# Layer 1's query projection: from fp32 to three fp32r products of split parts, with the first four tiles turned inside layer 0's feed-forward

## The chip, the core and the metric

The kernel runs on one NeuronCore of one Trainium2 chip. The core has five engines with a queue of instructions each: TensorE (PE; its weight loads are shown apart as PEld), VectorE (DVE), ScalarE (ACT), GpSimd (POOL) and SyncE (SP, which only issues DMAs here). They run side by side and wait for each other by semaphores. The metric is the device time of one execution in microseconds, as a median of several runs; less is better. A profile comes from one more execution, whose time is given beside its span.

## What is computed

Two layers work on x of 8 sequences x 112 rows x 512. Each layer adds a cross-attention to a context of 375 rows and then a gated feed-forward of width 1408. The change is about the queries of layer 1 alone:

```
x = x + L0_xattn(layernorm(x), ctx, mask)
x = x + L0_ffn(layernorm(x), w1, w2, w3)        # activations in 8 bits, weights ternary
x = x + L1_xattn(layernorm(x), ctx, mask, Wq, bq, Wk, bk, Wv, bv, Wo, bo, ...)
x = x + L1_ffn(layernorm(x), ...)               # weights are integers with a scale

# in L1_xattn
q = layernorm(x) @ Wq.T + bq                    # 896 x 512 by 512 x 512, fp32
k = ctx @ Wk.T + bk;  v = ctx @ Wv.T + bv       # 16 heads of 32
probs = softmax(clip(q k' / sqrt(32), -50, 50)) # masked
```

## The kernel before

The 8 x 112 rows are held in SBUF as 7 tiles of 128 rows, `xs[0]` to `xs[6]`. They form two groups, `GROUPS = [(0, 4), (4, 7)]`: tiles 0 to 3 (512 rows) and tiles 4 to 6 (384 rows).

Layer 0's feed-forward runs tile by tile (L561 to L611). `gate_up0(i)` (L509) makes both products from the quantized row tile in three pieces of H (512, 512, 384); ScalarE takes Silu (L521) and VectorE multiplies (L522). `ranges0(i)` finds the rows' scales: a square sum on ScalarE (L271), a maximum on VectorE (L272) and then a chain of some fifteen operations on one number per row (L275 to L282), each of which waits for the one before; its result is `q_fwd`. `round0(i)` (L541) scales on ScalarE (L543) and rounds on GpSimd in two halves (L546). `turn_down0(i)` transposes that on TensorE (L328) and copies it out on ScalarE (L330), and `down0(i)` (L553) multiplies by w3 and adds to `xs[i]` on VectorE (L559). The loop is skewed: tile i's gate_up0 stands ahead of tile i-1's turn_down0 and down0. `turn_gate0(i + 1)` transposes the next tile's quantized rows. Between these, `fill(n)` takes n steps of the keys and values of layer 1 (L181 and L190, fp32), which need only the context. A step ends with a copy out of PSUM: keys by ScalarE (L184), values by VectorE (L192).

What sets the order: TensorE and SyncE follow the order in which the program is written, everywhere. Up to `written.close()` (L612) VectorE, ScalarE and GpSimd do so too. What comes after L612 is put by a scheduler where it finds room, and can stand ahead of written code: the normalisations "ln2a" and "ln2b" of L614 and L620 appear in VectorE's queue from 145 us on.

After the loop come the queries of layer 1. `transpose2(i, ...)` (L205) writes the normalised tile `d` (L144), transposes it with four fp32 transposes (L214) and copies it by ScalarE into `h2T` (L215). `queries(g)` (L650) has four blocks `dc` of 128 outputs; each is four fp32 matmuls over the chunks `kc` of 128 inputs (L656), as wide as the group has rows, and an addition of bq on VectorE (L658) into `qT`. The order on TensorE is tiles 0 and 1, turn_down0(6), a fill, tiles 2 and 3, down0(6), then two blocks of group 0, tile 4, a block, tile 5, a block, tile 6, a fill, group 1's four blocks, and `fold_bias` (L670). Then the attention of layer 1 begins with `scores` (L811).

Memory: large tiles share seven slabs of 12 KB per partition (L71): raw weights, the quantized rows `h1`, keys and values of each sequence, `wq`, `h2T`, later the integers of layer 1's feed-forward. A slab is handed out again when its last reader is done. Layer 1's feed-forward (L935, L953) multiplies in fp32r, the type of which the change makes use; a value in it is split there into a rounded part and a rest (L753, L754 and L943, L944).

Of the kernel before, what the change touches and what calls it, by code (L numbers as in the profile page):

```python
# [42 lines left out]
NT = B * T // P  # L43
# [5 lines left out]
LN_EPS = 1e-5  # L49
# [10 lines left out]
HBLK = [(0, 512), (512, 512), (1024, 384)]  # L60


@with_exitstack
def two_layers(ctx: ExitStack, tc: tile.TileContext, x, ctxT, ctxN, mask0, mask1, w1, w2, w3,
               wq, wk, wv, wo, bq, bk, bv, bo, gamma, beta, rscale,
# [9 lines left out]
    def slab(name, dtype=F32):  # L75
        return slabs.tile([P, SLAB], dtype, name=name, tag="slab")
# [26 lines left out]

    small = [stat]

    def rsqrt(v, name):

        r, n = v.shape
        bits = small[-1].tile([P, n], I32, name=f"{name}_b", bufs=2)[:r]
        nc.vector.tensor_scalar(bits, v.bitcast(I32), 1, None, ALU.logical_shift_right)  # L110
        y = small[-1].tile([P, n], F32, name=f"{name}_y", bufs=2)[:r]
        nc.vector.tensor_scalar(y.bitcast(I32), bits, -1.0, RSQRT, ALU.mult, ALU.add)
        h = small[-1].tile([P, n], F32, name=f"{name}_h", bufs=2)[:r]
        nc.vector.tensor_scalar_mul(h, v, -0.5)
        t = small[-1].tile([P, n], F32, name=f"{name}_t", bufs=2)[:r]
        for _ in range(3):
            if n == 1:
                nc.vector.scalar_tensor_tensor(t, y, h, y, ALU.mult, ALU.mult)
            else:
                nc.vector.tensor_mul(t, y, y)  # L120
                nc.vector.tensor_mul(t, t, h)
            nc.vector.scalar_tensor_tensor(y, t, 1.5, y, ALU.add, ALU.mult)
        return y

    def moments(srcs, name):

        r = srcs[0].shape[0]
        mv = small[-1].tile([P, len(srcs), nc.vector.BN_AGGR_DIM], F32, name=f"{name}_mv", bufs=2)[:r]
        for j, src in enumerate(srcs):
            bn = small[-1].tile([P, nc.vector.BN_STATS_DIM], F32, name="bn", bufs=4)[:r]  # L130
            nc.vector.bn_stats(bn, src)
            nc.vector.bn_aggr(mv[:, j, :], bn)
        return mv

    def normaliser(srcs, name):

        mv = moments(srcs, name)
        r = srcs[0].shape[0]
        ve = small[-1].tile([P, len(srcs)], F32, name=f"{name}_ve", bufs=2)[:r]
# [58 lines left out]
    def fill(n=1):  # L198
        for _ in range(n):
            next(kv_steps, None)  # L200


    h2T = {}

    def transpose2(i, write, j, pool, psum):  # L205
        g = 0 if i < GROUPS[0][1] else 1
        i0, i1 = GROUPS[g]
        if i == i0:
            h2T[g] = slab("h2T")[:, :KC * (i1 - i0) * P].rearrange("p (k t) -> p k t", k=KC)
        h = pool.tile([P, D], F32, name="d", bufs=2)  # L210
        write(h, j)
        pt = psum.tile([P, KC, P], F32, name="s")
        for kc in range(KC):
            nc.tensor.transpose(pt[:, kc, :], h[:, kc * P:(kc + 1) * P], ident)  # L214
        nc.scalar.copy(h2T[g][:, :, (i - i0) * P:(i - i0 + 1) * P], pt)  # L215


    with tc.tile_pool(name="w0", bufs=1, side="right") as w0p, \
# [45 lines left out]
        def quantizers(srcs, n, name, squares):  # L264


            m = len(srcs)
            ss = w0p.tile([P, m], F32, name=f"{name}_ss", bufs=2)
            mx = w0p.tile([P, m], F32, name=f"{name}_mx", bufs=2)
# [7 lines left out]
            lim = w0p.tile([P, m], F32, name=f"{name}_lim", bufs=2)  # L277
            nc.vector.tensor_mul(lim, mx, r)
            nc.vector.tensor_scalar_max(lim, lim, Q_EPS)
            fwd = w0p.tile([P, m], F32, name=f"{name}_fwd", bufs=2)  # L280
            nc.vector.reciprocal(fwd, lim)
            nc.vector.scalar_tensor_tensor(fwd, fwd, 127.0, r, ALU.mult, ALU.mult)  # L282

            def back(mean, which):
                t = w0p.tile([P, m], F32, name=f"{name}_back{which}", bufs=4)
# [48 lines left out]
            q1[i] = transposed_h(q1[i], D, "q1", w0p)  # L334


        with tc.tile_pool(name="work0", bufs=2, side="right") as work0:
# [6 lines left out]

            def load_x(b0, b1):

                pool = w0p if b1 == B else work0
                t = pool.tile([T, b1 - b0, D], F32, name=f"x0_{b0}", bufs=1)
                nc.sync.dma_start(out=t, in_=x[b0:b1].rearrange("b t d -> t b d"))
                x0.extend(t[:, b, :] for b in range(b1 - b0))  # L350
# [155 lines left out]
        with tc.tile_pool(name="work1", bufs=2, side="right") as work1:  # L506
# [43 lines left out]
            def turn_down0(i):  # L550
                q3[i] = transposed_h(q3[i][0], H, "q3", work1), q3[i][1]
# [24 lines left out]
            ranges0(1, 1)  # L576
            round0(1)
            fill(1)
            for i in range(2, NT):
                gate_up0(i)  # L580
                if i == 2:
                    steps_of(2, 2)
                elif i == 3:
                    next(preparing[2])
                elif i == 4:
                    next(preparing[3])
                ranges0(i, 2)
# [36 lines left out]

# [25 lines left out]
    def queries(g):  # L650
        i0, i1 = GROUPS[g]
        cols = slice(i0 * P, i1 * P)
        for dc in range(KC):
            ps = ps_mm.tile([P, 512], F32, name="mm")[:, :(i1 - i0) * P]
            for kc in range(KC):
                nc.tensor.matmul(ps, lhsT=wq_s[:, kc, dc * P:(dc + 1) * P], rhs=h2T[g][:, kc, :],  # L656
                                 start=(kc == 0), stop=(kc == KC - 1))
# [25 lines left out]
    folding = fold_bias()  # L683
    next(folding)
    fill(1)
    for _ in queries(1):
        pass
    next(folding)
# [398 lines left out]
```

## Time and profile before

| what | us |
|---|---|
| median of three runs | 529.88 (529.83 to 530.57) |
| the profiled execution: its own time | 527.85 |
| the profiled execution: its span | 526.1 |
| mean granted clock of TensorE | 0.994 |
| L656, query products: start of the first to end of the last | 214.1 to 243.1 |
| idle ahead of L656 by the trace | 6.7, all of it weight loads waiting for their turn |
| tile 4 of layer 0's feed-forward: TensorE waits for VectorE's L316 | 1.75, at 177.4 |
| tile 3 of it: TensorE waits for VectorE's L559 | 0.73, at 150.1 |
| ScalarE ahead of L215 of tile 4: waits for L656 | 16.4, ended at 229.0 |

How to read a profile line: engine or start first, then the length in microseconds, the line of the kernel, the operation, what it writes and reads with its shape, and in brackets the idle time ahead of it with what ended it. An fp32 matmul leaves two records on TensorE, one in a shorter type leaves one. Consecutive instructions of one kind are merged ("x16"), and then the start of the next line tells better than the length when they were over. The chain of waits is followed back from the last instruction and lists the pieces of work that nothing could have shortened without something else coming last. GpSimd's times are rough.

### The profile page before, as it was taken

Reading aid. Unit: us, or ns where it says so; the run is one execution under the profiler, and the core shown is the slowest. Engines: PE = TensorE matmul, PEld = TensorE weight load, DVE = VectorE, ACT = ScalarE, POOL = GpSimd, SP = SyncE. Lnnn points to the kernel's source line nnn. Section 1 sums busy time; section 2 is a strip of 40 time slices with the busy share of each in tenths; the row PEclk is TensorE's granted clock in tenths of the full one; section 3 lists DMA queues with packets and bytes.
Section 4 is the critical chain, followed back from the end, with each engine's and each line's share of the span. In section 5 each row is a group of like instructions: output and inputs, shape, how many; then the busy total and the mean of one; then the engine's idle time right before and its main releaser. Section 6 shows DMA issues by size and latency. Waiting matters only on the chain.

```text
span 526.1 us, 8715 instructions
## 1 busy us (share of the span) xinstructions
PE 510.2 (97%) x3348; PEld 311.8 (59%) x3348; DVE 323.7 (62%) x797; ACT 246.4 (47%) x429; POOL 121.8 (23%) x218
## 2 busy tenths in 40 slices
PE   9999999999999899999989999999999999999994
PEld 6445554454554455455565465555554788889983
DVE  2552558767899767533566587796888763334432
ACT  0335747766755456013775365376565233103310
POOL 0000211111011111300551447447572430000000
PEclk9999999999999999999999999999999999999999
DMA  8998795100400100500430031011311000010001
GB/s 249 348 405 329 249 348 197 40 0 1 137 2 2 58 2 0 191 2 1 148 110 26 1 120 51 1 53 37 108 39 52 22 0 0 21 40 21 1 20 45
DMA packets 13231, 45.75 MB, mean 87 GB/s; under 512 B 1969, under 2 KB 3008, under 8 KB 12032
## 3 DMA queue, kind: packets, MB, share of 16 engines
q1 hardware_dynamic: 11744, 41.43, 23.0%
q0 software_dynamic: 1280, 3.70, 2.1%
q8 instruction: 28, 0.46, 0.3%
q14 instruction: 19, 0.16, 0.1%
q10 hardware_dynamic: 160, 0.01, 0.0%
HBM read 41.46 MB, written 1.84 MB: 82 GB/s over the span
## 4 chain that ended last, share of the span: by engine, by line
PE 81%; DVE 9%; ACT 3%; POOL 3%; DMA 2%; issue 1%; DVEq 0%; POOLq 0%; ACTq 0%
PE s L935 14%; PE mm L190 13%; PE mm L181 12%; PE down L953 7%; PE mm L517 5%; PE mm L656 5%; PE mm L407 4%; PE s L378 4%; PE mm L709 3%; PE s L811 3%; PE num L837 3%; PE mm L557 2%; PE den L832 2%; DVE e L816 2%; PE s L328 1%
## 5 line engine op out<-in xcount | busy, mean ns | idle before, releaser
L181 PE MATMUL mm<-cT,wk 128*128 128x375 f32 x256 | 88.2, 489 | 0.0
L190 PE MATMUL mm<-wv,cT 128*125 128x512 f32 x192 | 87.5, 599 | 0.0
L935 PE MATMUL s<-h4T,w 128*128 128x512 f32 (+1 forms) x352 | 72.6, 367 | 0.6 <-ACT qT L844 0.6
L816 DVE TENSOR_SCALAR e<-s,upper 125x448 f32<-125x448 f32 x96 | 59.2, 676 | 18.0 <-PE s L811 11.5
L935 PEld LDWEIGHTS s<-h4T,w 128*128 128x128 f32 x352 | 63.5, 188 | 9.2 <-PE num L837 0.9
L817 ACT ACTIVATE e<-e 125x448 f32<-125x448 f32 x96 | 52.3, 571 | 30.3 <-DVE e L816 29.7
L181 PEld LDWEIGHTS mm<-cT,wk 128*128 128x128 f32 x256 | 47.1, 192 | 28.2 <-issue 2.0
L190 PEld LDWEIGHTS mm<-wv,cT 128*125 128x125 f32 x192 | 34.5, 187 | 37.9 <-issue 36.4
L953 PE MATMUL down<-w,gu 128*128 128x512 f32 x154 | 37.0, 397 | 0.0
L517 PE MATMUL mm<-w_q,q_qT 128*128 128x512 fp8e4 (+1 forms) x168 | 34.6, 361 | 0.7 <-DVE tokens L559 0.7
L803 POOL TENSOR_TENSOR e<-e,e 125x448 f32<-125x448 f32 x28 | 32.2, 1181 | 10.9 <-PE num L837 10.9
L811 PE MATMUL s<-qT,kv 32*125 32x112 f32 x768 | 31.7, 283 | 2.5 <-DVE e L816 1.7
L788 POOL TENSOR_SCALAR w<-raw 128x640 fp32r<-128x640 int32 (+2 forms) x29 | 19.9, 690 | 56.4 <-ACT w L786 56.0
L953 PEld LDWEIGHTS down<-w,gu 128*128 128x128 f32 x154 | 28.7, 188 | 6.7
L546 POOL TENSOR_SCALAR q<-gu 128x704 bf16<-128x704 f32 x14 | 10.8, 791 | 93.1 <-ACT gu L543 93.1
L811 PEld LDWEIGHTS s<-qT,kv 32*125 32x125 f32 x768 | 26.1, 186 | 9.8 <-issue 5.5
L415 POOL DMA_DIRECT2D tokens<-x x14 | 10.7, 768 | 90.1 <-DVE x L409 62.1
L943 ACT CAST gu<-gu 128x512 fp32r<-128x512 f32 (+1 forms) x22 | 12.5, 568 | 40.0 <-DVE gu L941 40.0
L786 ACT ACTIVATE w<-raw,zero_point 128x640 fp32r<-128x640 int32 (+2 forms) x29 | 22.6, 779 | 17.1 <-DMA raw<-in_wd_dram 9.1
L941 DVE SCALAR_TENSOR_TENSOR gu<-s,su,gu 128x512 f32<-128x512 f32 (+1 forms) x22 | 15.0, 684 | 22.2 <-PE s L935 20.6
L517 PEld LDWEIGHTS <-q_qT 128*128 128x128 bf16 x168 | 16.4, 98 | 19.3 <-issue 2.1
L837 PEld LDWEIGHTS num<-e,kv 125*32 125x32 f32 x768 | 18.8, 110 | 12.8 <-issue 7.1
(211 smaller groups left out, 756.3 us busy)
## 6 DMA issues: line engine op xcount, KB each, us to landing
cT<-in_ctxT_dram SPq DMA_DIRECT2D x13, 750.0 KB, 6.7
raw<-in_w_dram SPq DMA_DIRECT2D x6, 1408.0 KB, 22.2
cN<-in_ctxN_dram SPq DMA_DIRECT2D x8, 768.0 KB, 4.9
raw<-in_wg_dram SPq DMA_DIRECT2D x8, 320.0 KB, 2.9
raw<-in_wu_dram SPq DMA_DIRECT2D x8, 320.0 KB, 3.0
raw<-in_wd_dram SPq DMA_DIRECT2D x8, 320.0 KB, 3.0
out_dram<-d SPq DMA_DIRECT2D x7, 256.0 KB, 2.0
wk<-in_wk_dram SPq DMA_DIRECT2D x4, 256.0 KB, 4.9
```

What stands on the lines that cost most here:

```text
L181: nc.tensor.matmul(ps[dc], lhsT=wk_s[:, kc, dc * P:(dc + 1) * P], rhs=cT[:, kc, :], start=(kc == 0), stop=(kc == KC - 1))
L190: nc.tensor.matmul(ps, lhsT=cT[:, kc, c * CK:(c + 1) * CK], rhs=wv_s[:, kc, :], start=(kc == 0), stop=(kc == KC - 1))
L517: nc.tensor.matmul(ps[:, :n], lhsT=qT[:, kc, :], rhs=w[:, kc * H + n0:kc * H + n0 + n], start=(kc == 0), stop=(kc == KC - 1))
L656: nc.tensor.matmul(ps, lhsT=wq_s[:, kc, dc * P:(dc + 1) * P], rhs=h2T[g][:, kc, :], start=(kc == 0), stop=(kc == KC - 1))
L786: nc.scalar.activation(t, raw, AF.Square, bias=zero_point, accum_out=squares[:, k:k + 1])
L803: add(e, e, e1)
L811: nc.tensor.matmul(ss[r][:, dc, :], lhsT=kT[rows, dc, c * CK:(c + 1) * CK], rhs=qT[rows, dc, b * T:(b + 1) * T], start=True, stop=True)
L816: nc.vector.tensor_scalar(e, ss[r], upper[:, c, b:b + 1], -CLIP, ALU.min, ALU.max)
L817: nc.scalar.activation(e, e, AF.Exp, scale=SC1)
L837: nc.tensor.matmul(num[r * HD:(r + 1) * HD, dc, :], lhsT=v[:, c, head], rhs=es[r][:CK, dc, :], start=(c == 0 and dc == 0), stop=(c == NCK ...
L935: nc.tensor.matmul(ps[:, :n], lhsT=w[:, c:c + P], rhs=h4T[k][:, kc, :n], start=(kc == 0 and k == 0), stop=(kc == KC - 1 and k == 1))
L953: nc.tensor.matmul(ps, lhsT=gus[k][:, hc, j * P:(j + 1) * P], rhs=w[:, c:c + D], start=(hc == 0 and k == 0), stop=(hc == HC - 1 and k == 1))
```

## The change

Each value of the transposed rows and of wq is split into a high part, rounded to fp32r after scaling by `LESS`, and a rest; a scaled difference of the two is a third operand. A block of queries is then high x high + low x low in one PSUM tile, and diff x diff in a second tile `less`, all fp32r: 12 matmuls for 4 fp32 ones. ScalarE takes the first tile out with scale and bias, VectorE subtracts the second.

wq is loaded one tile earlier (behind `i == 3`). At the end of tile 4 ScalarE makes `wq_high`, and GpSimd makes `wq_low` (128 x 2048, a subtraction and a scaling) and half of `wq_diff` (128 x 1024); the other half follows at the end of tile 5. The moments of tiles 0 to 3 are taken within the loop, their 1/std is worked out in tile 5 behind ranges0, and the transposes of tiles 0 and 1 stand at the end of tile 5, those of tiles 2 and 3 at the end of tile 6, ahead of turn_down0(6). All of this is in the written order. Group 1 stays behind the loop, with statistics for tiles 4 and 5 together. New buffers `wq_high`, `wq_low`, `h2T_high` and group 1's three parts get pools of their own; several small tiles get one buffer in place of two, and the last half of x moves to another pool.

```diff
+SPLIT = 2.0 ** -12
+LESS = 1.0 - 2.0 ** -13
...
-    def transpose2(i, write, j, pool, psum):
+    def write2(i, write, j, pool):
+        h2[i] = pool.tile([P, D], F32, name="d", bufs=2)
+        write(h2[i], j)
+
+    def transpose2(i, psum):
+
         g = 0 if i < GROUPS[0][1] else 1
...
         for kc in range(KC):
-            nc.tensor.transpose(pt[:, kc, :], h[:, kc * P:(kc + 1) * P], ident)
-        nc.scalar.copy(h2T[g][:, :, (i - i0) * P:(i - i0 + 1) * P], pt)
+            nc.tensor.transpose(pt[:, kc, :], h2[i][:, kc * P:(kc + 1) * P], ident)
+        j = i - GROUPS[g][0]
+        high, low, diff = (t[:, :, j * P:(j + 1) * P] for t in h2T[g])
+        nc.scalar.activation(high, pt, AF.Identity, scale=LESS)
+
+        def end():
+            nc.vector.tensor_sub(low, pt, high.bitcast(F32))
+            nc.vector.scalar_tensor_tensor(diff, high.bitcast(F32), SPLIT, low.bitcast(F32),
+                                           ALU.mult, ALU.subtract)
+        return end
...
-                pool = w0p if b1 == B else work0
+                pool = last0 if b1 == B else work0
...
+            mv2 = stat.tile([P, GROUPS[0][1], nc.vector.BN_AGGR_DIM], F32, name="mv2")
+
+            def moments2(i):
+                bn = stat.tile([P, nc.vector.BN_STATS_DIM], F32, name="bn", bufs=4)
+                nc.vector.bn_stats(bn, xs[i])
+                nc.vector.bn_aggr(mv2[:, i, :], bn)
+
+            def difference():
+
+                t = slab("h2T", F32R)
+                k = len(wq_diff) * KC // 2
+                kcs = slice(k, k + KC // 2)
+                wq_diff.append(t[:, KC * D:].rearrange("p (k d) -> p k d", d=D))
+                nc.gpsimd.tensor_sub(wq_diff[-1], wq_high[:, kcs].bitcast(F32),
+                                     wq_low[:, kcs].bitcast(F32))
+                return t[:, :KC * D].rearrange("p (k t) -> p k t", k=KC)
+
+            ending2 = []
             for i in range(2, NT):
                 gate_up0(i)
...
                 ranges0(i, 2)
                 if i == 4:
                     next(preparing[3])
+                    moments2(0)
+                    moments2(2)
+                elif i == 5:
+                    small.append(stat)
+                    ve = stat.tile([P, GROUPS[0][1]], F32, name="ln2a_ve")
+                    nc.vector.tensor_scalar_add(ve, mv2[:, :, 1], LN_EPS)
+                    rstd2 = rsqrt(ve, "ln2a")
+                    small.pop()
+
+                    def normal2(h, i):
+                        nc.vector.tensor_scalar(h, xs[i], mv2[:, i, 0:1], rstd2[:, i:i + 1],
+                                                ALU.subtract, ALU.mult)
+                    for k in range(2):
+                        write2(k, normal2, k, work1)
                 fill(2 if i < 4 else 1)
                 turn_down0(i - 1)
...
+                elif i == NT - 1:
+                    for k in range(2):
+                        ending2[k]()
+                        write2(k + 2, normal2, k + 2, work1)
                 fill(1)
                 if i < NT - 1:
                     turn_gate0(i + 1)
...
                 down0(i - 1)
                 if i == 3:
                     next(preparing[3])
-                if i == 4:
                     wq_s = slab("wq")[:, :KC * D].rearrange("p (k d) -> p k d", k=KC)
                     nc.sync.dma_start(out=wq_s, in_=wq)
+                    moments2(1)
+                elif i == 4:
+                    queried = ExitStack()
+                    qp = queried.enter_context(tc.tile_pool(name="qp", bufs=1))
+                    wq_high, wq_low, h2T_high = (qp.tile([P, KC, D], F32R, name=name)
+                                                 for name in ("wq_high", "wq_low", "h2T_high"))
+                    nc.scalar.activation(wq_high, wq_s, AF.Identity, scale=LESS)
+                    nc.gpsimd.tensor_sub(wq_low, wq_s, wq_high.bitcast(F32))
+                    nc.gpsimd.tensor_scalar(wq_low, wq_low.bitcast(F32), 1.0 / SPLIT, 1.0,
+                                            ALU.mult, ALU.mult)
+                    wq_diff = []
+                    h2T_diff = difference()
+                    moments2(3)
+                elif i == 5:
+                    h2T[0] = h2T_high, difference(), h2T_diff
+                    ending2 += [transpose2(k, ps_s) for k in range(2)]
+                elif i == NT - 1:
+                    ending2 += [transpose2(k, ps_s) for k in range(2, 4)]
+                    ending2[2]()
+                    ending2[3]()
+            turn_down0(NT - 1)
+            fill(1)
             written.close()
             small.pop()
-            write = normaliser(xs[:3], "ln2a")
-            for i in range(2):
-                transpose2(i, write, i, work1, ps_s)
-            turn_down0(NT - 1)
-            fill(1)
-            transpose2(2, write, 2, work1, ps_s)
-            write = normaliser(xs[3:5], "ln2b")
-            transpose2(3, write, 0, work1, ps_s)
             down0(NT - 1)
...
             for kc in range(KC):
-                nc.tensor.matmul(ps, lhsT=wq_s[:, kc, dc * P:(dc + 1) * P], rhs=h2T[g][:, kc, :],
+                nc.tensor.matmul(ps, lhsT=wq_high[:, kc, of], rhs=high[:, kc, :],
+                                 start=(kc == 0), stop=False)
+                nc.tensor.matmul(ps, lhsT=wq_low[:, kc, of], rhs=low[:, kc, :],
+                                 start=False, stop=(kc == KC - 1))
+            less = ps_s.tile([P, 512], F32, name="s")[:, :(i1 - i0) * P]
+            for kc in range(KC):
+                nc.tensor.matmul(less, lhsT=wq_diff[kc // 2][:, kc % 2, of], rhs=diff[:, kc, :],
                                  start=(kc == 0), stop=(kc == KC - 1))
-            nc.vector.tensor_scalar_add(qT[:, dc, cols], ps, bq_s[:, dc:dc + 1])
+            nc.scalar.activation(qT[:, dc, cols], ps, AF.Identity, bias=bq_s[:, dc:dc + 1],
+                                 scale=1.0 + SPLIT)
+            nc.vector.tensor_sub(qT[:, dc, cols], qT[:, dc, cols], less)
             yield
...
-    transpose2(4, write, 1, tailp, ps_s)
-    next(asking)
-    for i in range(5, NT):
-        transpose2(i, normaliser(xs[i:i + 1], f"ln2{i}"), 0, tailp, ps_s)
-        next(asking, None)
...
+        write = normaliser(xs[4:6], "ln2b")
+        for i in range(4, NT):
+            if i == NT - 1:
+                write = normaliser(xs[i:], "ln2c")
+            write2(i, write, i % 2, tailp)
+            transpose2(i, ps_s)()
+            next(asking, None)
```

More of the change, by code (lines that the diff above doesn't have):

```diff
@@ L104, in two_layers, with buffers @@
     small = [stat]
+    def buffers(name):
+        return 2 if name in ("q3", "ln3") else 1
     def rsqrt(v, name):
         r, n = v.shape
-        bits = small[-1].tile([P, n], I32, name=f"{name}_b", bufs=2)[:r]
+        bufs = buffers(name)
+        bits = small[-1].tile([P, n], I32, name=f"{name}_b", bufs=bufs)[:r]
         nc.vector.tensor_scalar(bits, v.bitcast(I32), 1, None, ALU.logical_shift_right)
-        y = small[-1].tile([P, n], F32, name=f"{name}_y", bufs=2)[:r]
+        y = small[-1].tile([P, n], F32, name=f"{name}_y", bufs=bufs)[:r]
         nc.vector.tensor_scalar(y.bitcast(I32), bits, -1.0, RSQRT, ALU.mult, ALU.add)
-        h = small[-1].tile([P, n], F32, name=f"{name}_h", bufs=2)[:r]
+        h = small[-1].tile([P, n], F32, name=f"{name}_h", bufs=bufs)[:r]
         nc.vector.tensor_scalar_mul(h, v, -0.5)
-        t = small[-1].tile([P, n], F32, name=f"{name}_t", bufs=2)[:r]
+        t = small[-1].tile([P, n], F32, name=f"{name}_t", bufs=bufs)[:r]
         for _ in range(3):
@@ L127, in moments @@
         r = srcs[0].shape[0]
-        mv = small[-1].tile([P, len(srcs), nc.vector.BN_AGGR_DIM], F32, name=f"{name}_mv", bufs=2)[:r]
+        mv = small[-1].tile([P, len(srcs), nc.vector.BN_AGGR_DIM], F32, name=f"{name}_mv",
+                             bufs=buffers(name))[:r]
         for j, src in enumerate(srcs):
@@ L138, in normaliser @@
         r = srcs[0].shape[0]
-        ve = small[-1].tile([P, len(srcs)], F32, name=f"{name}_ve", bufs=2)[:r]
+        ve = small[-1].tile([P, len(srcs)], F32, name=f"{name}_ve", bufs=1)[:r]
         nc.vector.tensor_scalar_add(ve, mv[:, :, 1], LN_EPS)
@@ L200, in fill @@
             next(kv_steps, None)
-    h2T = {}
-    def transpose2(i, write, j, pool, psum):
-        g = 0 if i < GROUPS[0][1] else 1
[L207 to L211, printed above, removed]
+    h2T, h2 = {}, {}
+    def write2(i, write, j, pool):
+        h2[i] = pool.tile([P, D], F32, name="d", bufs=2)
+        write(h2[i], j)
+    def transpose2(i, psum):
+        g = 0 if i < GROUPS[0][1] else 1
         pt = psum.tile([P, KC, P], F32, name="s")
         for kc in range(KC):
-            nc.tensor.transpose(pt[:, kc, :], h[:, kc * P:(kc + 1) * P], ident)
-        nc.scalar.copy(h2T[g][:, :, (i - i0) * P:(i - i0 + 1) * P], pt)
+            nc.tensor.transpose(pt[:, kc, :], h2[i][:, kc * P:(kc + 1) * P], ident)
[7 more added lines that the diff above has]
+        return end
     with tc.tile_pool(name="w0", bufs=1, side="right") as w0p, \
@@ L267, in quantizers @@
             m = len(srcs)
-            ss = w0p.tile([P, m], F32, name=f"{name}_ss", bufs=2)
-            mx = w0p.tile([P, m], F32, name=f"{name}_mx", bufs=2)
+            ss = w0p.tile([P, m], F32, name=f"{name}_ss", bufs=buffers(name))
+            mx = w0p.tile([P, m], F32, name=f"{name}_mx", bufs=buffers(name))
             for j, src in enumerate(srcs):
@@ L276, in quantizers @@
             r = rsqrt(ss, name)
-            lim = w0p.tile([P, m], F32, name=f"{name}_lim", bufs=2)
+            lim = w0p.tile([P, m], F32, name=f"{name}_lim", bufs=buffers(name))
             nc.vector.tensor_mul(lim, mx, r)
             nc.vector.tensor_scalar_max(lim, lim, Q_EPS)
-            fwd = w0p.tile([P, m], F32, name=f"{name}_fwd", bufs=2)
+            fwd = w0p.tile([P, m], F32, name=f"{name}_fwd", bufs=buffers(name))
             nc.vector.reciprocal(fwd, lim)
@@ L284, in back @@
             def back(mean, which):
-                t = w0p.tile([P, m], F32, name=f"{name}_back{which}", bufs=4)
+                t = w0p.tile([P, m], F32, name=f"{name}_back{which}",
+                             bufs=4 if name == "q3" else 1)
                 nc.vector.tensor_scalar(t, lim, mean, 1.0 / 127.0, ALU.mult, ALU.mult)
@@ L334, in turn_gate0 @@
             q1[i] = transposed_h(q1[i], D, "q1", w0p)
-        with tc.tile_pool(name="work0", bufs=2, side="right") as work0:
+        with tc.tile_pool(name="work0", bufs=2, side="right") as work0, \
+                tc.tile_pool(name="last0", bufs=1, side="right") as last0:
             m0 = load(work0, mask0, [B, S2], "m0", nc.scalar, U8)
@@ L652, in queries @@
         cols = slice(i0 * P, i1 * P)
+        high, low, diff = h2T[g]
         for dc in range(KC):
+            of = slice(dc * P, (dc + 1) * P)
             ps = ps_mm.tile([P, 512], F32, name="mm")[:, :(i1 - i0) * P]
             for kc in range(KC):
-                nc.tensor.matmul(ps, lhsT=wq_s[:, kc, dc * P:(dc + 1) * P], rhs=h2T[g][:, kc, :],
+                nc.tensor.matmul(ps, lhsT=wq_high[:, kc, of], rhs=high[:, kc, :],
[5 more added lines that the diff above has]
+                nc.tensor.matmul(less, lhsT=wq_diff[kc // 2][:, kc % 2, of], rhs=diff[:, kc, :],
                                  start=(kc == 0), stop=(kc == KC - 1))
-            nc.vector.tensor_scalar_add(qT[:, dc, cols], ps, bq_s[:, dc:dc + 1])
+            nc.scalar.activation(qT[:, dc, cols], ps, AF.Identity, bias=bq_s[:, dc:dc + 1],
+                                 scale=1.0 + SPLIT)
+            nc.vector.tensor_sub(qT[:, dc, cols], qT[:, dc, cols], less)
             yield
@@ L677, in two_layers @@
     next(asking)
-    transpose2(4, write, 1, tailp, ps_s)
-    next(asking)
-    for i in range(5, NT):
-        transpose2(i, normaliser(xs[i:i + 1], f"ln2{i}"), 0, tailp, ps_s)
-        next(asking, None)
[L683 to L688, printed above, removed]
+    with tc.tile_pool(name="g1p", bufs=1, side="right") as g1p:
+        h2T[1] = [g1p.tile([P, KC, 384], F32R, name=f"h2T1_{k}") for k in range(3)]
+        write = normaliser(xs[4:6], "ln2b")
[5 more added lines that the diff above has]
+            next(asking, None)
+        folding = fold_bias()
+        next(folding)
+        fill(1)
+        for _ in queries(1):
+            pass
+        next(folding)
+    queried.close()
+    tail2 = ctx.enter_context(tc.tile_pool(name="tail2", bufs=1, side="right"))
     sg_s = load(tailp, sg, [P, HC], "sg", nc.gpsimd)
     su_s = load(tailp, su, [P, HC], "su", nc.gpsimd)
-    h4T = [tailp.tile([P, KC, 512], F32R, name=f"h4T_{k}") for k in range(2)]
+    h4T = [tail2.tile([P, KC, 512], F32R, name=f"h4T_{k}") for k in range(2)]
     h4 = {}
```

## The prediction

> **What bounds the kernel now.** I read the page first, then the chain of waits around the queries, then the timelines of each engine over the last feed-forward tiles. From the page:
>
> ```profile
> PE 510.2 (97%) x3348; PEld 311.8 (59%) x3348; DVE 323.7 (62%) x797; ACT 246.4 (47%) x429; POOL 121.8 (23%) x218
> ...
> PE 81%; DVE 9%; ACT 3%; POOL 3%; DMA 2%; issue 1%; DVEq 0%; POOLq 0%; ACTq 0%
> ```
>
> TensorE is the bound nearly everywhere. The chain from 200 to 245 us (start, length, piece) holds nothing but TensorE:
>
> ```profile
> 211.92 2.37 PE mm L557 x11
> 214.29 6.87 PE mm L656 x16
> ...
> 225.47 3.44 PE mm L656 x8
> ...
> 232.78 10.32 PE mm L656 x32
> ```
>
> So what the queries lose in TensorE time the kernel gains, as long as no new wait stands in front. The waits must be sought in the tiles before, where the change puts its preparation. There, in the old order, VectorE and GpSimd (start, length):
>
> ```profile
> 160.16 0.77 DVE L121 TENSOR_TENSOR ln_t<-ln_t,ln_h 128x2 f32<-128x2 f32 x1
> 160.96 0.71 DVE L122 SCALAR_TENSOR_TENSOR ln_y<-ln_t,ln_y 128x2 f32<-128x2 f32 x1
> 161.71 0.16 DVE L120 TENSOR_TENSOR ln_t<-ln_y 128x2 f32<-128x2 f32 x1
> ...
> 189.77 0.16 DVE L282 SCALAR_TENSOR_TENSOR q_fwd<-q_fwd,q_y 128x1 f32<-128x1 f32 x1
> ...
> 193.26 0.75 DVE L559 SCALAR_TENSOR_TENSOR tokens<-mm,q_back,tokens 128x512 f32<-128x512 f32 x1 [3.20 <-PE mm L557]
> ```
>
> ```profile
> 160.14 1.52 POOL L546 TENSOR_SCALAR q<-gu 128x704 bf16<-128x704 f32 x2 [14.15 <-ACT gu L543]
> ...
> 191.74 1.52 POOL L546 TENSOR_SCALAR q<-gu 128x704 bf16<-128x704 f32 x2 [11.43 <-ACT gu L543]
> ```
>
> Two operations of 2 elements, worth 0.15 us, took 0.77 and 0.71: each ended with one of GpSimd's two 0.76 us instructions. One VectorE operation got in per GpSimd instruction, no more.
>
> **The queries.** Every fp32 product of L656 is two records. A block of group 0 is 8 records in 3.44 us; four blocks are 6.87 + 3.44 + 3.44 = 13.75. Group 1 is 10.32. The new products are fp32r, the type of layer 1's feed-forward, one record each:
>
> ```profile
> 417.32 34.15 PE L935 MATMUL s<-h4T,w 128*128 128x512 f32 x144
> ...
> 473.17 30.69 PE L935 MATMUL s<-h4T,w 128*128 128x384 f32 x176
> ```
>
> By the starts of what follows (451.31 and 503.70) they go at 33.99/144 = 0.236 and 30.53/176 = 0.1735 us, each with its own weight load. A group has 4 blocks x 4 chunks x 3 products = 48: 11.33 and 8.33. Gain: 2.42 + 1.99 = **4.4 us**. Transposes are as many as before (28), and down0, fill and turn_down0 keep their number.
>
> **The rest of the query stage: 0.** Counted from the first query at 0, block 0 ends at 2.8, block 1 at 5.6, tile 4's transposes at 6.1. The first eviction needs bq, which landed 5.2 us in (L658 at 219.31 waited for it) and frees block 0's bank before 6.1. VectorE has, up to tile 6's parts: the residual 0.75, two normal writes 1.1, statistics and rsqrt of tile 6 3.2, its write 0.5, four subtractions of `less` 2.8, three ends of 1.45, some 12.7 us; they must be over when group 1 begins at 11.3 + 1.3 + 3.4 = 16.0 (fold_bias's 2.8 can follow, it is needed 8.3 later). The cover is 3 us; a bad order of VectorE's free schedule costs up to 1. ScalarE sat idle 16.4 us here before and takes the evictions and fp32r copies (0.6 each). The last subtraction of `less` (0.6 to 0.7, as L658's 0.62) lies beside L670's 0.86.
>
> **Moved off older tiles: -0.9.** The old ln2a work had floated forward: a bn_stats of 0.59 at 145.29, two d writes (0.46 each) at 171.24 and a statistic at 168.05. Behind the first, TensorE waited 0.73 until L559 at 149.33; without it the quantizer's chain can start when ScalarE's accumulator is there, 146.17, not 146.47: 0.3. Behind the others, TensorE waited 1.75 for L316 before tile 5's transposes; the chain gets some 0.9 shorter of which 0.3 is the shift itself: 0.6. The new moments of tiles 0 and 2 come behind L316 and delay only PSUM copies that have about 0.5 us to spare. The wq load moves up one tile in SP's queue; it already went at 140.60, with only context loads beside it: 0.
>
> **Tile 5: +5.0, the step that decides.** All on the old clock, less 0.9. wq_high (128x2048 on ScalarE, by L543's 1.56 for 1408 about 2.1) fills an idle stretch, 178.2 to 180.3; gate_up0(5)'s first L521 behind it comes 0.1 late, and a free PSUM pair covers that. Then GpSimd gets three long instructions in one go: a subtraction of 2048, a scaling of 2048, a subtraction of 1024. By L788 (0.40 for 256, 0.73 for 640) the scaling takes 1.95. [...] The quantizer's chain of tile 5 reaches its first two-input operation at 187.0 and was worth 2.1 more. [...]
>
> ```profile
> 409.41 1.30 POOL L722 TENSOR_TENSOR tokens<-tokens,beta 128x512 f32<-128x512 f32 x1
> ```
>
> ```profile
> 409.84 1.35 DVE L850 TENSOR_TENSOR qT<-qT,e 128x448 f32<-128x448 f32 x1
> ```
>
> (L850 alone: 0.62; it ran from 410.57.) [...] Tile 1's transposes end at 197.8 to 198.2. Queued behind them on TensorE is gate_up0(6), which without waits would start at 183.85 + 2.53 + 0.61 + 2.58 + 0.22 + 2.37 + 0.87 = 193.05. That is 5.0. Lower end: 2.8 if both writes pass ahead of the second difference; 0.3 if the chain isn't held either.
>
> **Tile 6: +0.8.** L559 and the quantizer first; then two ends (0.67 + 0.75) and two writes before down0(5)'s result. Tile 3's d is ready some 1 us after TensorE asks, also with GpSimd's pair in between; behind it stands turn_down0(6), which had 0.16 to wait for GpSimd anyway. From 0.4 to 1.2.
>
> **The clock: +1.7.** A gap has a second price here (columns: PE, PEld, DVE, ACT, POOL busy, granted clock, DMA share, GB/s):
>
> ```profile
> 271.00:272.00 1.00, 0.00 (x0) 0.00 (x0) 0.89 (x2) 0.00 (x0) 0.99 (x1) 1.00 0.07 23
> 272.00:273.00 1.00, 0.53 (x3) 0.36 (x3) 1.00 (x3) 0.66 (x2) 1.00 (x2) 1.00 0.36 117
> ...
> 275.00:276.00 1.00, 1.00 (x15) 0.81 (x9) 0.41 (x1) 0.16 (x2) 1.00 (x2) 0.50 0.06 16
> 276.00:277.00 1.00, 1.00 (x2) 0.62 (x3) 1.00 (x3) 0.67 (x2) 0.82 (x2) 0.50 0.00 0
> ```
>
> After 1.7 us idle and some thin work the clock was halved for 3.4 us: 1.7 lost. [...]
>
> **Other edits: 0.** The smaller buffer counts are of names allocated once. x's last half in its own pool and the new pools only move addresses; a release waited for would cost up to 1 us, and nothing suggests a gain.
>
> **Sum.** -4.4 - 0.9 + 5.0 + 0.8 + 1.7 = +2.2: from the profiled execution's 527.85 (span 526.1 and 1.75 around it) to 530.05. The median of the runs is 2.03 above that execution; 529.88 + 2.2 = **532.1**.
>
> **The rivals.** (A) The forecast, chance 0.54, 530.9 to 534.2. (B) The same hold, but no dip behind it, or the old dip gone: +0.5, 530.4; chance 0.14. (C) Faster: GpSimd lets VectorE's two writes through ahead of the second difference. [...] For it: TensorE needs only two writes, 0.92 us. Against it: the alternation at 160.16. [...] Chance 0.23. (D) The lock hardly bites, long GpSimd work lies beside VectorE: -4.4 - 0.9 + 0.3 + 0.4 = -4.6, 525.3; speaks against it that L850 was held for nearly all of 1.3 us. Chance 0.09. That fp32r doesn't reach its rate is covered by L953, which loads other weights every time and takes 0.233.
>
> **How the numbers follow.** 0.2% is 1.06 us, about what a measurement here can tell from no change. Slower: nearly all of A and a little of B, 0.55. Same: most of B and the upper part of C, 0.18. Faster: D and most of C, 0.27. The range from 527.4 to 534.2 leaves out D, a strip of C and a strip above A.
>
> **What would show it.** Right: L656's successor takes 11.3 and 8.3 us; VectorE's small operations beside GpSimd's long ones last 2 us and more; TensorE sits idle about 5 us between tile 5's down0 and tile 6's gate_up0, with a clock of 0.5 behind it. Wrong: TensorE dense there; or a wait in the query stage, on bq or VectorE, of over 1 us.

## The result and the profile after

The changed kernel took 530.95 us (median of 21 runs) beside 529.41 us of the kernel before: ratio 1.0035, interval 1.002 to 1.005, so it is slower, by 1.1 to 2.7 us. The forecast was 532.1, a ratio of 1.0042, within 527.4 to 534.2. The profiled execution grew from 526.1 to 528.5 us of span.

The page first: busy time of each engine, and the shares of the chain that ended last.

```profile
PE 508.7 (96%) x3380; PEld 319.5 (60%) x3380; DVE 339.7 (64%) x801; ACT 252.7 (48%) x438; POOL 132.4 (25%) x222
...
PE 84%; DVE 11%; ACT 1%; DMA 1%; issue 1%; SPq 0%; DVEq 0%; ACTq 0%
```

TensorE is busy 1.5 us less than before in a span that is 2.4 us longer: it stands idle for longer, and VectorE's share of the chain rose from 9 to 11%. TensorE's timeline names the places (start, length, group, idle time before it and what ended that):

```profile
189.90 2.54 PE L579 MATMUL mm<-w_q,q_qT 128*128 128x512 fp8e4 x11
197.10 1.94 PE L226 MATMUL s<-ident,d 128*128 128x128 f32 x8 [4.67 <-DVE d L641]
198.84 6.39 PE L539 MATMUL mm<-w_q,q_qT 128*128 128x512 fp8e4 x24
...
214.65 0.63 PE L226 MATMUL s<-ident,d 128*128 128x128 f32 x4 [0.89 <-DVE d L641]
...
221.40 0.58 PE L730 MATMUL mm<-h2T_high,wq_high 128*128 128x512 f32 x1
...
228.17 0.50 PE L730 MATMUL mm<-h2T_high,wq_high 128*128 128x512 f32 x1 [0.52 <-ACT qT L738]
...
247.50 1.14 PE L899 MATMUL s<-qT,kv 32*125 32x112 f32 x32
```

The same places in the kernel before:

```profile
190.69 2.54 PE L557 MATMUL mm<-w_q,q_qT 128*128 128x512 fp8e4 x11
193.06 4.92 PE L517 MATMUL mm<-w_q,q_qT 128*128 128x512 fp8e4 x24
...
205.91 1.04 PE L214 MATMUL s<-ident,d 128*128 128x128 f32 x8
...
214.13 7.03 PE L656 MATMUL mm<-h2T,wq 128*128 128x512 f32 x16
...
243.88 1.14 PE L811 MATMUL s<-qT,kv 32*125 32x112 f32 x32
```

Three waits are new: 4.67 us ahead of the transposes of tiles 0 and 1 (L226), 0.89 ahead of those of tile 3, and 0.52 within the queries. GpSimd and VectorE show the making of the first:

```profile
180.21 4.53 POOL L677 TENSOR_TENSOR wq_low<-wq,wq_high 128x2048 fp32r<-128x2048 f32 x1 [0.69 <-ACT wq_high L676]
184.83 1.90 POOL L678 TENSOR_SCALAR wq_low<-wq_low 128x2048 fp32r<-128x2048 f32 x1
186.82 2.42 POOL L615 TENSOR_TENSOR h2T<-wq_high,wq_low 128x1024 fp32r<-128x1024 f32 x1
192.86 1.51 POOL L568 TENSOR_SCALAR q<-gu 128x704 bf16<-128x704 f32 x2 [3.62 <-ACT gu L565]
194.34 2.33 POOL L615 TENSOR_TENSOR h2T<-wq_high,wq_low 128x1024 fp32r<-128x1024 f32 x1
```

```profile
187.07 2.18 DVE L129 SCALAR_TENSOR_TENSOR q_t<-q_y,q_h 128x1 f32<-128x1 f32 x1
189.28 0.16 DVE L133 SCALAR_TENSOR_TENSOR q_y<-q_t,q_y 128x1 f32<-128x1 f32 x1
...
193.01 0.62 DVE L132 TENSOR_TENSOR ln2a_t<-ln2a_t,ln2a_h 128x4 f32<-128x4 f32 x1
193.67 0.71 DVE L133 SCALAR_TENSOR_TENSOR ln2a_y<-ln2a_t,ln2a_y 128x4 f32<-128x4 f32 x1
194.42 3.00 DVE L641 TENSOR_SCALAR d<-tokens,mv,ln2a_y 128x512 f32<-128x512 f32 x2
```

And the four writes of d by themselves (least, median and greatest length in ns):

```profile
L641 DVE TENSOR_SCALAR d<-tokens,mv,ln2a_y x4: 534/537/2541, 194.4 to 214.0; 128x512 f32<-128x512 f32 x4
```

L129 on one column (0.22 us at 189.48, with nothing beside it) took 2.18: it ended with GpSimd's first `difference` at 189.24. Five microseconds on, the two writes of d took 3.00 together, where 1.00 is what they take with little beside them (below). It was the first of them that was held: it started at 194.42, 0.08 after the second `difference`, and took 2.54, to 196.96; the `difference` ended at 196.67. The second write followed in 0.54. Not all of VectorE was held: L292, which reads one operand, took 1.62 beside L678 (184.88 to 186.50), as in the second kernel below with GpSimd idle, and L123 and L125 took 0.15 and 0.14 beside the first `difference`. What followed the wait ran at half clock, a granted clock of 0.50 (columns as before: PE, PEld, DVE, ACT, POOL busy, granted clock, DMA share, GB/s):

```profile
194.00:195.00 1.00, 0.00 (x0) 0.00 (x0) 0.96 (x2) 0.00 (x0) 1.00 (x2) 0.99 0.00 0
195.00:196.00 1.00, 0.00 (x0) 0.00 (x0) 1.00 (x1) 0.00 (x0) 1.00 (x1) 0.50 0.00 0
...
200.00:201.00 1.00, 1.00 (x4) 0.33 (x3) 0.00 (x0) 0.21 (x1) 0.00 (x0) 0.50 0.00 0
201.00:202.00 1.00, 1.00 (x4) 0.37 (x3) 0.00 (x0) 0.47 (x1) 0.00 (x0) 0.59 0.00 0
202.00:203.00 1.00, 1.00 (x6) 0.49 (x5) 0.65 (x1) 0.00 (x0) 0.00 (x0) 1.00 0.00 0
```

The scores (L811 before, at 243.88; L899 now) start at 247.50, 3.6 us later. This is the sum: down0(4) ends 0.8 earlier (193.06 before, the start of the next matmul, 2.37 behind its own; 189.90 + 2.37 = 192.27 now), the wait adds 4.67, half clock 2.3 (the eight transposes 1.94 for 1.04, the 24 gate_up matmuls 6.39 for 4.92), tile 6 1.1 (0.89 of it the wait for tile 3's d), and queries to scores take 26.10 (221.40 to 247.50) for 29.75 (214.13 to 243.88), 3.65 less: -0.8 + 4.67 + 2.3 + 1.1 - 3.65 = 3.6. Starts and modelled ends are mixed here, so a single term is good to about 0.2. From the scores to the end it is 281.0 us now and was 282.2.

### The profile page after: what moved, and what is told of

Read it like the earlier page. It is cut to its first block, busy times and chain, and to the rows that moved or that the text cites. A ratio compares the mean times of both kernels' runs of the same rounds, so it can differ in the third digit from the quotient of the medians.

```text
span 528.5 us, 8781 instructions
## 1 busy us (share of the span) xinstructions
PE 508.7 (96%) x3380; PEld 319.5 (60%) x3380; DVE 339.7 (64%) x801; ACT 252.7 (48%) x438; POOL 132.4 (25%) x222
## 4 chain that ended last, share of the span: by engine, by line
PE 84%; DVE 11%; ACT 1%; DMA 1%; issue 1%; SPq 0%; DVEq 0%; ACTq 0%
PE mm L202 14%; PE s L1023 14%; PE mm L193 13%; PE down L1041 7%; PE s L899 5%; PE mm L539 5%; PE mm L797 5%; PE mm L429 4%; PE s L400 4%; PE num L925 3%; PE den L920 3%; PE mm L579 1%; DVE e L904 1%; DVE q_mx L292 1%; DVE q_t L129 1%
## 5 line engine op out<-in xcount | busy, mean ns | idle before, releaser
L539 PE MATMUL mm<-w_q,q_qT 128*128 128x512 fp8e4 (+1 forms) x168 | 36.1, 372 | 0.4 <-DVE tokens L581 0.4
L899 PE MATMUL s<-qT,kv 32*125 32x112 f32 x768 | 31.8, 286 | 2.2 <-DVE e L904 1.7
L899 PEld LDWEIGHTS s<-qT,kv 32*125 32x125 f32 x768 | 26.4, 188 | 9.2 <-issue 4.8
```

The source lines that it names most:

```text
L539: nc.tensor.matmul(ps[:, :n], lhsT=qT[:, kc, :], rhs=w[:, kc * H + n0:kc * H + n0 + n], start=(kc == 0), stop=(kc == KC - 1))
L899: nc.tensor.matmul(ss[r][:, dc, :], lhsT=kT[rows, dc, c * CK:(c + 1) * CK], rhs=qT[rows, dc, b * T:(b + 1) * T], start=True, stop=True)
```

## The experiments

Two accounts stood against each other. The theory, which the expectations call the lock: GpSimd's long instructions hold VectorE's two-input operations and the writes of d (L129 took 2.18 us for 0.22, a write 2.54 for 0.54); the wait that this makes ahead of tile 0's transposes, and the half clock behind it, eat what the queries gain. The rivals: the transposes themselves, moved into the feed-forward, cost the time; or the gap costs what it shows and the clock nothing.

**Where GpSimd's work stands.** Two kernels move a part of it. The first puts the second half's difference on VectorE:

```diff
-                nc.gpsimd.tensor_sub(wq_diff[-1], wq_high[:, kcs].bitcast(F32),
-                                     wq_low[:, kcs].bitcast(F32))
+                engine = nc.vector if k else nc.gpsimd
+                engine.tensor_sub(wq_diff[-1], wq_high[:, kcs].bitcast(F32),
+                                  wq_low[:, kcs].bitcast(F32))
```

> The changed kernel with the second half of the weights' difference (128x1024) on VectorE instead of GpSimd, behind tile 4's residual. Theory (the lock): nothing of GpSimd stands behind round0(5)'s pair, so the first write of d no longer waits 2.5 us; tile 0's transposes start near 195 instead of 197.1 and TensorE's gap is 2.7 instead of 4.7; if that is short enough the clock stays up. 2 to 4.5 us less than the changed kernel: 526.5 to 529. Rival (the gap comes from the length of VectorE's own queue, not from GpSimd): VectorE gets 1.1 us more work, the gap stays at 4.7, the time at 531 to 532.

Measured: 526.77 us, ratio 0.9955 (0.9942 to 0.9969). TensorE and VectorE there:

```profile
195.68 1.09 PE L226 MATMUL s<-ident,d 128*128 128x128 f32 x8 [2.67 <-DVE d L642]
196.60 4.92 PE L539 MATMUL mm<-w_q,q_qT 128*128 128x512 fp8e4 x24
```

```profile
187.64 2.18 DVE L129 SCALAR_TENSOR_TENSOR q_t<-q_y,q_h 128x1 f32<-128x1 f32 x1
...
194.99 1.00 DVE L642 TENSOR_SCALAR d<-tokens,mv,ln2a_y 128x512 f32<-128x512 f32 x2
```

```profile
196.00:196.50 0.50, 0.50 (x7) 0.46 (x6) 0.50 (x2) 0.15 (x1) 0.00 (x0) 1.00 0.00 0
```

The writes fell from 3.00 to 1.00 and the gap from 4.67 to 2.67, the same 2.00; L129 is still held 2.18, since the first three instructions stayed. In this execution no slice at half clock follows. That 2.67 us of idle never brings it is not shown: 8 of this kernel's 19 executions had a mean clock of 0.987 or 0.988, the other 11 of 0.990 or 0.991, and the 67 executions of the kernels below in which the gap is under 1 us or filled never less than 0.989. One stretch of 3.4 us at half clock, as attention had before, is by an estimate (half of 3.4 over 525) 0.003 of the mean, and the 8 took 1.4 us more (medians 527.7 and 526.3); where it fell in them no trace shows. Counted from down0(4), the scores start 5.1 us earlier than in the changed kernel: 2.0 of gap, 2.3 of clock and 0.8 of a query wait that is gone here too (25.26 from queries to scores, for 26.10). The ratio fell by 0.0080, 4.2 us; some of the 5.1 is given back behind the scores.

The second kernel takes the scaling to ScalarE, in tile 5, and with it both differences behind the writes of d:

```diff
-                    nc.gpsimd.tensor_scalar(wq_low, wq_low.bitcast(F32), 1.0 / SPLIT, 1.0,
-                                            ALU.mult, ALU.mult)
-                    wq_diff = []
-                    h2T_diff = difference()
...
                 elif i == 5:
+                    nc.scalar.activation(wq_low, wq_low.bitcast(F32), AF.Identity,
+                                         scale=1.0 / SPLIT)
+                    wq_diff = []
+                    h2T_diff = difference()
```

> The changed kernel with the scaling of wq_low on ScalarE at the end of tile 5, and both halves of the difference behind it on GpSimd, so that two of GpSimd's three long instructions move from beside VectorE's chains to beside tile 6's matmuls. Theory (the lock): the quantizer's first link of 2.18 us and the write of 2.54 us go back to 0.2 and 0.5; TensorE's gap shrinks from 4.7 to under 1 us and the half clock behind it goes: 4 + 2.3 = 6 to 7 us less than the changed kernel, 524 to 525, some 1% under the kernel before. Rival (the early turning itself, that is rstd2 and the writes behind the quantizer, makes the gap): 2 us of gap and the half clock stay, 528 to 530.

Measured: 524.17 us, ratio 0.991 (0.9892 to 0.9929); run once more in a later batch, 524.43, 0.9915 (0.9893 to 0.9937):

> The scaling of Wq's low part on ScalarE after both halves' products, both differences then on GpSimd, once more, as the partner of the run below. 0.991 of the kernel before, 0.989 to 0.993.

Its TensorE, VectorE and GpSimd (first run):

```profile
193.44 1.08 PE L226 MATMUL s<-ident,d 128*128 128x128 f32 x8 [0.78 <-DVE d L641]
```

```profile
187.29 0.22 DVE L129 SCALAR_TENSOR_TENSOR q_t<-q_y,q_h 128x1 f32<-128x1 f32 x1
```

```profile
193.86 4.78 POOL L615 TENSOR_TENSOR h2T<-wq_high,wq_low 128x1024 fp32r<-128x1024 f32 x2 [1.15 <-ACT wq_low L680]
```

L129 is back at 0.22 and the gap at 0.78. The 4.67 us are so taken apart: 2.00 by the second difference, 1.89 by the hold of L129 (the scaling and the first difference moved away; the subtraction of 2048 stayed and ends at 184.96, before the chain starts), 0.78 by the writes and the new rstd2 themselves. The 4.78 us of GpSimd are still there, beside gate_up0(6), and cost nothing that shows. Against the first kernel the scores start 1.8 earlier, counted from down0(4), which is the gap's 1.9; the ratio fell by 0.0045, 2.4 us, with intervals of 0.7 us and more on each side.

**The turning alone.** The early transposes stay, the queries are fp32 as before, and the split isn't made:

```diff
-        nc.scalar.activation(high, pt, AF.Identity, scale=LESS)
...
+        nc.scalar.copy(h2T[g][:, :, j * P:(j + 1) * P], pt)
+        return lambda: None
...
-                nc.tensor.matmul(ps, lhsT=wq_high[:, kc, of], rhs=high[:, kc, :],
-                                 start=(kc == 0), stop=False)
...
+                nc.tensor.matmul(ps, lhsT=wq_s[:, kc, of], rhs=h2T[g][:, kc, :],
```

> One part alone: the first four tiles turned within the last tiles of layer 0, as in the changed kernel, but with fp32 queries: no split of wq, no ends, no GpSimd work beyond round0. Theory (the split's GpSimd work makes the loss): tile 5's chain runs at its own 2.1 us, TensorE's gap in front of gate_up0(6) is under 0.7, tile 3's transposes hardly wait; 0.9 is won on older tiles and up to 0.7 lost here: 528.5 to 529.5, at the kernel before's time. Rival (the turning makes it): a gap of 2 us and more, 531 and above.

Measured: 528.83 us, ratio 0.999 (0.9976 to 1.0003).

```profile
193.32 1.08 PE L226 MATMUL s<-ident,d 128*128 128x128 f32 x8 [0.78 <-DVE d L635]
```

The same 0.78, without any of GpSimd's new work. The rival that the moved transposes are the cost falls: they are worth between -0.24% and +0.03%.

**The clock.** Twenty fp32 matmuls of `ones` by `ones`, which nobody reads, fill the gap and leave its length alone:

```diff
                 elif i == 5:
                     h2T[0] = h2T_high, difference(), h2T_diff
+                    busy = ps_s.tile([P, P], F32, name="s")
+                    for _ in range(20):
+                        nc.tensor.matmul(busy, lhsT=ones, rhs=ones, start=True, stop=True)
```

> The changed kernel with 20 products of ones by ones (fp32, 128 columns, result unused) on TensorE between tile 5's down0 and the transposes of tiles 0 and 1, some 4.3 us of work within the 4.7 us gap. Theory (the gap has a second price through the clock): the gap's length stays, but the clock is 1.0 behind it, so the transposes take 0.9 and gate_up0(6) 4.75 instead of 1.74 and 6.2: 2.3 us less than the changed kernel, about 528.6. Rival (the lower clock in the records costs nothing, the pieces are slow for another reason, or the clock is lowered later all the same): the same time as the changed kernel or up to 0.5 more.

Measured: 528.45 us, ratio 0.9984 (0.9973 to 0.9996). Timeline, then windows:

```profile
192.51 4.63 PE L687 MATMUL s<-ones 128*128 128x128 f32 x40
197.40 1.08 PE L226 MATMUL s<-ident,d 128*128 128x128 f32 x8 [0.26 <-DVE d L641]
```

```profile
196.00:197.00 1.00, 1.00 (x11) 0.95 (x9) 1.00 (x1) 0.00 (x0) 0.97 (x1) 1.00 0.00 0
...
199.00:200.00 1.00, 1.00 (x6) 0.46 (x5) 0.40 (x2) 0.77 (x2) 0.00 (x0) 1.00 0.00 0
```

The transposes start 197.40, as late as ever, and the kernel is 0.0051 (2.7 us) faster: the clock stays at 1.00, the transposes take 1.08 and gate_up0(6) 4.92, which is the 2.3 us of the clock. Counted from down0(4), the scores start only 1.6 earlier, as bq is later still here (26.71 from queries to scores, for 26.10); the rest is gained behind the scores. So the gap had a second price here, 2.3 us, and it came with TensorE idle and not with TensorE at work, behind the same wait.

**The third wait, and the best version.** To the second kernel, both writes in tile 6 ahead of both ends (an end is the `end()` of the change: VectorE makes `low` and `diff` of a turned tile):

```diff
                     for k in range(2):
-                        ending2[k]()
                         write2(k + 2, normal2, k + 2, work1)
+                    for k in range(2):
+                        ending2[k]()
```

> The kernel with the scaling on ScalarE, and in tile 6 both writes of d ahead of both ends. Theory: the 0.94 us that TensorE waits for tile 3's d in front of turn_down0(6) is VectorE's order (write, end, write, with GpSimd's pair in between); with the writes first it is gone, 0.9 us less than the kernel with the scaling on ScalarE: 523.3. Rival: turn_down0(6) then waits for GpSimd's pair, which VectorE's ends hold up, and nothing or up to 0.3 is won: 523.9 to 524.2.

Measured: 521.85 us (5 runs), ratio 0.9845 (0.9822 to 0.9867). That is more than the wait could explain, so both kernels were run again on one chip:

> As the run above, with tile 6's two writes of d ahead of both ends of the older tiles. Theory: the only thing that it takes away is tile 6's wait of 0.94 us for tile 3's d, so 0.9 us (0.0018) below the run above, ratio about 0.989. If what the first run showed beyond that holds (0.9845 against 0.991): 3 us or more below the run above, and then there is a second gain that the trace must name.

Measured: 523.02, ratio 0.9896 (0.9867 to 0.9925), 1.4 us below its partner. In the second profile:

```profile
207.03 1.04 PE L226 MATMUL s<-ident,d 128*128 128x128 f32 x8
```

The eight transposes run in one go; the 0.94 us for tile 3's d is gone. Counted from down0(4), the scores start 1.13 earlier than in the partner. The second pair agrees with the theory (0.0019 for 0.0018), but the intervals of the two overlap, so it is the trace that shows this gain and not the times. The first pair's excess did not come back. This version is 1.0 to 1.6% under the kernel before, and under the changed kernel by 1.4% where the two ran side by side.

**bq.** ScalarE's first eviction of queries stood behind a 2 KB load:

```profile
227.43 1.27 ACT L738 ACTIVATE qT<-mm,bq 128x512 f32<-128x512 f32 x2 [10.23 <-DMA bq<-in_bq_dram]
```

It arrived 6.0 us into the queries; before, 5.2; in the first two kernels above, 4.1. GpSimd issued it late, at 225.4, and it landed 1.9 later: by the trace behind an operation on group 1's statistics (L129) in the changed kernel, behind down0(6)'s residual (L581) in those two. What decides that was not settled. The changed kernel with bq loaded at the start:

```diff
+    bq_s = kvp.tile([P, KC], F32, name="bq")
...
+            nc.scalar.dma_start(out=bq_s, in_=bq)
...
-    bq_s = load(tailp, bq, [P, KC], "bq", nc.gpsimd)
```

> The changed kernel with bq loaded at the start of the kernel, on ScalarE's queue behind bk, into a place of its own. Theory: the 0.52 us that TensorE waits inside the queries comes from bq's late transfer alone, and it goes; nothing else moves: 530.4, 0.5 less than the changed kernel. Rival (VectorE's queue is the real limit there, and bq only the last of several): the wait stays or moves by a block: 530.9 to 531.

Measured: 530.51 us, ratio 1.0007 (0.9989 to 1.0025). Tile 4's to tile 5's transposes are 3.2 us apart, not 3.95, so the wait is gone; but from tile 6's transposes to the scores it is 13.69 us for 13.31, and queries to scores shrink only by 0.22 (25.88 for 26.10). What came back is a wait for the last part of group 1's rows, which VectorE writes: here `low` of tile 6 is done at 237.96 and the first product that reads it starts at 238.02. Another execution of the unchanged new kernel shows it by name:

```profile
238.47 0.44 PE L732 MATMUL mm<-h2T,wq_low 128*128 128x384 f32 x1 [0.35 <-DVE h2T L232]
```

By the ratio this run is 0.0028 (1.5 us) below the changed kernel, with intervals that touch; the trace up to the scores supports 0.2 us of that. So the time lies near the theory's 530.4, but the trace shows the rival: the wait moved. That the number fits is luck.

**A larger dose.** The second half's difference is made twice (the same values are written again):

```diff
+                for _ in range(1 + k // 2):
+                    nc.gpsimd.tensor_sub(wq_diff[-1], wq_high[:, kcs].bitcast(F32),
+                                         wq_low[:, kcs].bitcast(F32))
```

> The changed kernel with the second half of the weights' difference made twice on GpSimd, the same values written again (2.4 us of GpSimd work more, behind the first). Theory (the lock, one instruction of VectorE per boundary): one of the two writes of d passes between the two, the other waits for the end of the second; tile 0's transposes then start at about 197 as before and tile 1's at about 199.5, gate_up0(6) 2 to 2.4 us later, with the clock still at half: 532.5 to 533.5. Rival (the gap isn't GpSimd's doing): no change, 531.

Measured: 531.4 us, ratio 1.0033 (1.0015 to 1.005): no slower than the changed kernel, a miss. The trace did what was expected; TensorE, VectorE, GpSimd:

```profile
197.88 0.96 PE L226 MATMUL s<-ident,d 128*128 128x128 f32 x4 [4.63 <-DVE d L642]
200.43 1.08 PE L226 MATMUL s<-ident,d 128*128 128x128 f32 x4 [1.58 <-DVE q_back L307]
201.30 6.68 PE L539 MATMUL mm<-w_q,q_qT 128*128 128x512 fp8e4 x24
```

```profile
195.19 5.09 DVE L642 TENSOR_SCALAR d<-tokens,mv,ln2a_y 128x512 f32<-128x512 f32 x2
```

```profile
195.12 4.88 POOL L616 TENSOR_TENSOR h2T<-wq_high,wq_low 128x1024 fp32r<-128x1024 f32 x2
```

Each write now waits for one difference (5.09 us for the two): tile 0's transposes come where they came before, tile 1's 1.58 later. Counted from down0(4), gate_up0(6) starts 10.59 in and not 8.94. To see where that goes, the dose and the changed kernel were run again on one chip:

> The changed kernel once more, beside the three below on one chip, so that their ratios share the same runs of the kernel before. Both theories: 1.0035 of the kernel before, 1.002 to 1.005.

> The second half's difference made twice, as before (the second writes the same values again). In the trace of its first run tile 6's gate_up matmuls came 1.65 us later, counted from down0(4), than in the changed kernel. If the time of the gap goes on to the end: 1.0035 + 0.0031 = 1.0065 of the kernel before, and above the changed kernel of this batch by 1.2 to 2.2 us. If the rest of the program absorbs a late start here (and the first run's 1.0033 was no scatter): within 0.5 us of the changed kernel.

Measured: 531.75 us and 1.004 (1.002 to 1.0061) for the changed kernel, 531.21 and 1.004 (1.0024 to 1.0056) for the dose. In these traces gate_up0(6) is again 1.68 later (10.63 for 8.95) and takes 6.48, not 5.49, at half clock, 2.67 in all; but the scores come only 1.04 later (58.56 after down0(4) begins, for 57.52). The other 1.63 are waits of the changed kernel that the dose hasn't: tile 4's to tile 5's transposes are 3.18 apart, not 4.17 (bq), and tile 6's to the scores 13.25, not 13.89 (group 1's rows). The remaining 1.0 us is no larger than the intervals. So the hold is shown to grow with the dose (the two writes took 3.00 us and 5.09 with it); that the time does is not shown.

The pair shows why a microsecond is hard to tell here. Windows of the changed kernel's second execution:

```profile
196.00:197.00 1.00, 0.00 (x0) 0.00 (x0) 1.00 (x1) 0.00 (x0) 1.00 (x1) 0.99 0.00 0
197.00:198.00 1.00, 0.50 (x3) 0.53 (x4) 1.00 (x4) 0.00 (x0) 0.07 (x1) 0.50 0.00 0
...
200.00:201.00 1.00, 1.00 (x5) 0.44 (x4) 0.00 (x0) 0.20 (x2) 0.00 (x0) 0.81 0.00 0
201.00:202.00 1.00, 1.00 (x7) 0.42 (x5) 0.16 (x1) 0.56 (x1) 0.00 (x0) 1.00 0.00 0
```

Half clock for 3.4 us, from 197.0 (by the share of half clock in the last slice, 0.38, to 200.4), where the first execution had 6.8, from 195.0 to 201.8 (0.82 of the slice at 201), behind the same gap of 4.68. In attention, slices of half a microsecond give 6.8 in the first and 3.4 in the second. Within one batch, the changed kernel's two executions of mean clock 0.991 took 529.2 and 529.4 us, the seven at 0.984 to 0.985 530.7 to 533.8.

## Why the forecast was right, step by step

- **Queries, -4.4: right.** A block of group 0 takes 2.72 us, twelve products at 0.227; one of group 1 takes 2.11. Where no wait falls between, as in the second kernel, queries to scores take 25.26 (215.51 to 240.77), 4.49 less than before.
- **The rest of the query stage, 0: too low by 0.8.** bq was taken to land 5.2 us in, in time for block 0's bank; it landed 6.0 in. The bound of up to 1 held it. Taking this wait away gained 0.22 from queries to scores, as group 1's rows were next.
- **Older tiles, -0.9: measured -0.8**, by down0(4)'s end: the wait at tile 3 fell from 0.73 to 0.43, that at tile 4 from 1.75 to 1.26. The turning alone, at 0.999, doesn't contradict it.
- **Tile 5, +5.0: measured 4.67**, by the hold that before's rows show at 0.76 us an instruction (L121 and L122 at 160.16) and that now lasted for whole instructions of 2.4 us: L129, one small operation to each GpSimd boundary (L132, L133), and a write of d, the first, behind the second difference. That tile 1's transposes would end at 197.8 to 198.2, the term behind the 5.0, no run shows: it was the author's estimate, with 4.8 and 2.4 us for GpSimd's subtractions of 2048 and 1024. In the profiled execution these took 4.53, 2.42 and 2.33, and the transposes, at half clock, ended at 199.0. Rival C needed both writes to pass ahead of the second difference: neither did, as L133 took the boundary at the end of GpSimd's pair (194.38) and the first write then started 0.08 after the second difference. The terms of gate_up0(6)'s start without waits add up to 193.03, not 193.05, which changes nothing.
- **Tile 6, +0.8: measured 0.89** at L226.
- **The clock, +1.7: measured 2.3.** The term that was mis-sized: I priced 3.4 us of half clock, the length of before's dip in attention, with TensorE at work throughout; the profiled execution had 6.8, of which TensorE worked 4.7 (197.1 to 201.8), and half of 4.7 is 2.35. A second execution had 3.4, of which it worked 2.9: 1.5 (0.9 in the transposes, 0.57 in gate_up). Of the changed kernel's 21 executions in the result, 13 had a mean clock of 0.984 or 0.985 and took 530.3 to 533.0 us, and 8 had 0.987 to 0.993 and took 528.5 to 530.5. How long a gap must be to bring half clock is not shown. In the changed kernel it began 2.5 us after down0(4)'s last record (192.44 to 195.0), in the profiled execution of the first experiment 2.67 us of idle brought none, and the mean clocks of that experiment's other executions speak for a dip in some of them (0.987 or 0.988 in 8 of 19).
- **Not in the sum: -1.2 from the scores to the end.** Waits of 0.28, 0.80 and 0.63 us in the later stages (at 317, 381 and 406 of before) shrank to a single one of 0.21, while the attention dip lasted 6.8 us instead of 3.4. In the second execution, with a dip of 3.4 as before, it is 279.9, so -2.3. Which of these belong to the change and which to the execution is open; no run was made for it.

The sum of the parts was +2.2, the spans differ by 2.4 and the ratio gives 1.9 (1.1 to 2.7). The median of before shown at first (529.88) was 0.5 above that of the runs beside the change, a good third of the 1.15 that lie between 532.1 and 530.95. That the total came so close is in part luck: up to the scores the parts make 3.6 and not 2.2, as the clock cost 0.6 more and the queries gained 0.75 less than forecast, and the 1.2 gained behind the scores stood in no term. Rival D's 525.3 is about what the second kernel reached, 524.2, by moving the work and not by a lock that hardly bites.

## What to carry to other kernels

A GpSimd instruction of two to five microseconds wasn't free here, idle as GpSimd was: one of 2.42 held a one-column operation of VectorE for 2.18. Ask which VectorE operations stand beside such an instruction, and put it where VectorE has no chain that TensorE waits for; here putting 4.8 us of it behind two writes of d and giving 1.9 to ScalarE was worth 0.0125 of the time, and turned slower into faster. Price a gap on TensorE twice, by its length and by the clock behind it, and measure the second price: behind 4.67 us of idle it was 2.3 here, behind 2.67 nothing in the profiled execution, though perhaps 1.4 in others. Where a wait is removed, look for the next late operand: bq's 0.75 us gave 0.22.

## What the runs showed of the hardware that was not expected

- Behind one and the same gap (4.67 and 4.68 us), half clock lasted 6.8 us in one execution and 3.4 in another. In attention, half clock began behind 1.68 us idle (1.73 before), less than the 2.67 us that brought none in the first experiment's profiled execution: in these runs the length of one idle stretch alone didn't say where it fell.
- A stretch of half clock began within the gap: at 195.0, 2.5 us after TensorE's last record, with TensorE idle until 197.1. Only the part in which TensorE worked cost time: half of 4.7 us is 2.35, and 2.3 were lost.
- Matmuls that nobody reads kept the clock at 1.00 over 4.6 us. The transposes and gate_up0(6) behind them took 2.3 us less, and the time fell by 2.7.
